# Statistics of the first mamba block's layer norm, pinned behind the projection of the second block

## The chip, the cores and the metric

The kernel runs on one core of a Trainium2 chip. The metric is the time on the device in microseconds (us) of one launch; runs are given with their median. A core has five engines with queues of their own, each of which executes in order: TensorE (PE in the profile, its weight loads PEld), VectorE (DVE), ScalarE (ACT), GpSimd (POOL) and SyncE (SP), which here mostly issues DMA transfers. Engines wait for each other by semaphores. Matmuls write into PSUM, of which the kernel uses eight banks of 128 x 512 float32 in turn.

## The reference

Two sequences of 1024 tokens with 512 features pass four layers. After each, the input is added and the row normalised. The first layer is a Mamba-2 mixer; only it and its layer norm matter here:

```python
def _layernorm(x, axis=-1, eps=1e-05):
    m = jnp.mean(x, axis=axis, keepdims=True)
    v = jnp.var(x, axis=axis, keepdims=True)
    return (x - m) / jnp.sqrt(v + eps)
...
zxbcdt = jnp.einsum('bld,di->bli', hidden_states, W_in)     # gate, xBC, dt
xBC = jax.nn.silu(conv)                                     # causal, 4 taps
h = h * dA_t[:, :, None, None] + (dt_t[:, :, None] * x_t)[..., None] * B_t[:, None, None, :]
y = jnp.einsum('bhpn,bn->bhp', h, C_t)                      # one scan step
y = y * jax.nn.silu(gate)
y = y * jax.lax.rsqrt(var + EPS) * norm_w
return jnp.einsum('bld,do->blo', y, W_out)
...
x = _layernorm(x + _L0_attn_ref(x, ...), axis=-1)
x = _layernorm(x + _L0_ffn_ref(x, ...), axis=-1)
x = _layernorm(x + _L1_attn_ref(x, ...), axis=-1)           # gated linear recurrence
x = _layernorm(x + _L1_ffn_ref(x, ...), axis=-1)            # SwiGLU
```

## The kernel before

The 2048 tokens are worked on in four blocks of 512 (`TB`). A block's rows `X[b]` lie as four tiles of 128 tokens by 512 features (`NJ` = 4). The mamba layer of a block has these stages, each a Python generator whose steps are woven together:

- `head(b)` makes `xT`, the block with features on partitions. For blocks 2 and 3 a DMA brings blocks of 32 x 32 and VectorE turns them (`turn_blocks`, L270, four instructions). Then `pbc` (L387) projects to B, C and dt, ScalarE copies the result, VectorE convolves it, and a DMA lays dt out by rows (`turn`, L404) for the softplus chain.
- `project(b)` makes the inner channels `px` (L366), convolves them on VectorE (L292, three taps each), and makes the decay matrices `L`: ScalarE copies a row-broadcast decay into a PSUM bank `pl` (L566), and VectorE scans it (L572). GpSimd multiplies by the Gram matrix (L587).
- `recur(b)` goes over four chunks of 128 tokens: transposes `pxt` (L668), their product with dt `dtx` (L670), the outputs `py` (L691 from the state, L699 from inside the chunk), the new state `pst` and `H` (L709, L716, L723), and the sum into `xc` (L730).
- `gates(b)` makes the eight gate projections `pg`; `gate(b)` applies them.
- `conclude(b)` projects to the output (`po`, L764, one group of 16 TensorE instructions for each 128 tokens), adds the residual (L779), and at its end normalises the block (`layernorm`) and stores it (`store_rows`).

`layernorm` issues for each of four tiles a statistics instruction on VectorE (L279, `bn_stats`) and one that turns it into mean and variance (L280, `bn_aggr`); then a square root on ScalarE (L282), a reciprocal (L283) and four instructions (x - mean) * rs on VectorE (L285).

The blocks overlap: `conclude(0)` is the filling between the steps of `project(1)`, and what is left of it is woven into `recur(1)`, together with the gates of block 1 and the head of block 2:

```python
fill, plan = conclude(b - 1, before), (0, 0, 2, 0, 2, 0, 2, 2)
...
weave(project(b, st), fill, plan, rest=False)
weave(recur(b, H, st), alternate(itertools.chain(fill, g), ahead), (3,) * NJ)
```

The order on each engine is not the order of these calls. Only the very first part is in the written order (`manual_schedule`); otherwise a scheduler places instructions by its own costs, and may bring one forward as soon as its inputs are there. An instruction given to `tc.keep_in_program_order` stays behind what was issued before it on its engine and is not brought forward. The four transposes of `xT` in `head` are such instructions (`pinned=True`).

Of the kernel before, what the change touches and what calls it, by code (L numbers as in the profile page):

```python
# [18 lines left out]
NJ = TB // P  # L19
# [18 lines left out]
def model_kernel(ctx: ExitStack, tc: tile.TileContext, t: dict, out: bass.AP):  # L38
    nc = tc.nc
# [20 lines left out]
    def bank(name):  # L60
        return ps.tile([P, 512], F32, tag="mm", name=name)
# [17 lines left out]
    def tokens():  # L79
        return op.tile([P, NJ, D], F32, tag="x", name="x", bufs=3)  # L80

    X = [tokens() for _ in range(3)]
# [170 lines left out]
    def store_rows(rows, x):  # L253
        nc.sync.dma_start(rows.rearrange("(j p) d -> p j d", p=P), x)
# [16 lines left out]
            if pinned:  # L271
                tc.keep_in_program_order(turned)

    def layernorm(x, n=NJ, engine=nc.vector):

        mv = sp.tile([P, NJ, 2], F32, tag="mv", name="mv")
        for j in range(n):
            st = sp.tile([P, 6], F32, tag="st", name="st", bufs=4)
            nc.vector.bn_stats(st, x[:, j, :])  # L279
            nc.vector.bn_aggr(mv[:, j, :], st)  # L280
        rs = sp.tile([P, NJ, 1], F32, tag="rs", name="rs")
        nc.scalar.activation(rs[:, :n], mv[:, :n, 1:2], AF.Sqrt, bias=eps)  # L282
        nc.vector.reciprocal(rs[:, :n], rs[:, :n])  # L283
        for j in range(n):
            engine.tensor_scalar(  # L285
                x[:, j, :], x[:, j, :], mv[:, j, 0:1], rs[:, j, :], ALU.subtract, ALU.mult
            )

# [467 lines left out]
    def conclude(b, st):  # L756


        xc, sums = st["xc"], st["sums"]
        rms = sp.tile([P, NJ], F32, tag="rms", name="rms")  # L760
        for j in range(NJ):
            po = bank("po")
            for m in range(NX):
                nc.tensor.matmul(  # L764
                    po, xc[:, m, j * P : (j + 1) * P], w_out[:, m, :],
                    start=(m == 0), stop=(m == NX - 1),
                )
                if m == NX // 2 - 1:
                    yield
            if j == 0:  # L770
                pss = bank("pss")
                for i in range(NJ):
                    nc.tensor.matmul(
                        pss[:, i : i + 1], sums[:, i * P : (i + 1) * P], ones,
                        start=True, stop=True,
                    )
                nc.scalar.activation(rms, pss[:, :NJ], AF.Sqrt, bias=eps, scale=1.0 / DI)
                nc.vector.reciprocal(rms, rms)
            nc.vector.scalar_tensor_tensor(  # L779
                X[b][:, j, :], po, rms[:, j : j + 1], X[b][:, j, :], ALU.mult, ALU.add  # L780
            )
            yield
        layernorm(X[b])
        store_rows(x_mid[b], X[b])

    def by_blocks(b, st):
# [4 lines left out]
    H, before, st = None, None, {}  # L791
# [10 lines left out]
    for b in range(NBLK):  # L802
        if b:
            g, coming = gates(b, st), {}
            fill, plan = conclude(b - 1, before), (0, 0, 2, 0, 2, 0, 2, 2)
            ahead = iter(())
            if b + 1 < NBLK:
                by_blocks(b + 1, coming)
                ahead = head(b + 1, coming)
            weave(project(b, st), fill, plan, rest=False)  # L810

            weave(recur(b, H, st), alternate(itertools.chain(fill, g), ahead), (3,) * NJ)
        else:
            turns = (ahead, g, ahead, g, g, g, ahead)
            weave(recur(b, H, st), (next(steps, None) for steps in turns), (2, 2, 1, 2))
            for m in range(NX):
                tc.keep_in_program_order(nc.gpsimd.tensor_scalar(
                    w_out[:, m, :], w_out[:, m, :], normw[:, m : m + 1], 1.0, ALU.mult, ALU.mult
                ))
        H = st["H"]  # L820
        gate(b, st)
        before, st = st, coming
    before_last.close()
    last = (conclude(NBLK - 1, before), first_layer.close)


# [39 lines left out]
    def later_layers(exact, last=None):  # L866
# [82 lines left out]
        def linear(b):  # L949
# [41 lines left out]
            for j in range(NJ):  # L991
                nc.vector.scalar_tensor_tensor(
                    X[b][:, j, :], o[:, j, :], f[:, j : j + 1], X[b][:, j, :],
                    ALU.mult, ALU.add,
                )
            layernorm(X[b], engine=nc.gpsimd)
            if b:
                store_rows(x_lin[b], X[b])
# [44 lines left out]
        with tc.tile_pool(name="rec" + suffix, bufs=1, side="right", reuse_waits="tile") as rp:  # L1043
# [91 lines left out]
            def project_back(b, y):  # L1135
                for j in range(NJ):
                    po = bank("po")
                    for k in range(NK):
                        nc.tensor.matmul(  # L1139
                            po, y[:, k, j * P : (j + 1) * P], w1[4][:, k, :],  # L1140
                            start=(k == 0), stop=(k == NK - 1),
                        )
                    r = rp.tile([P, D], F32, tag="t2", name="r1", bufs=4)
                    nc.vector.tensor_tensor(r, po, bout, ALU.add)
                    nc.gpsimd.tensor_tensor(X[b][:, j, :], X[b][:, j, :], r, ALU.add)  # L1145

                if b + 1 < NBLK:
                    layernorm(X[b])
                    store_rows(x_rec[b], X[b])
# [277 lines left out]
```

## Time and profile before

| | |
|---|---|
| median of 3 runs | 1121.71 us (1121.63 to 1123.01) |
| the profiled execution | 1122.32 us, its span 1120.5 us |
| PE busy | 1102.6 us, 98% of the span |
| DVE busy | 704.6 us, 63% |
| ACT, POOL busy | 453.6 us and 366.5 us |
| mean granted TensorE clock | 0.997 |

Times in the profile are microseconds from the start of the span, which is from the first to the last instruction. A row of the timeline gives start, duration, engine, line and operation, then the tiles written and read, the shapes and how many instructions are merged into it; in brackets, how long the engine stood idle before it and whose work ended that. `conclude(0)` ends within 111 and 171 us: the statistics of this layer norm stand at 136.5, 138.1, 154.5 and 163.4, and its last normalising instruction just before 170.7.

### The profile page before, as it was taken

The page shows a single profiled execution, that of the slowest core. Times are in us where ns is not written, and L with a number is a line of the kernel's source. Part 1 is how long each engine was busy: PE and PEld are TensorE (multiplying, and loading weights), DVE is VectorE, ACT ScalarE, POOL GpSimd, SP SyncE. Part 2 cuts the span into 40 slices and gives each one's busy share as a digit, 9 for nine tenths or more (in the row PEclk, how much of TensorE's full clock was granted, in tenths as well). Part 3 has the DMA queues.
Part 4 walks back from the last instruction along what each step waited for, and adds up shares of the span by engine and source line. Part 5 has one row for each costly group of instructions (what it writes and reads, how often), then busy time and mean ns, then how long its engine had stood idle before and what let it go on. Part 6 is the DMA issues. An engine that isn't in the chain of part 4 may idle for free.

```text
span 1120.5 us, 12075 instructions
## 1 busy us (share of the span) xinstructions
PE 1102.6 (98%) x4450; PEld 664.5 (59%) x4450; DVE 704.6 (63%) x1266; ACT 453.6 (40%) x692; POOL 366.5 (33%) x347
## 2 busy tenths in 40 slices
PE   9999999999999999999999999999999999999996
PEld 5455445445544555645444444447888888888885
DVE  5989897697869676874646438184238865325224
ACT  3334633463454233556644372553223224224223
POOL 1547471465248340453433231236411001001000
PEclk9999999999999999999999999999999999999999
DMA  9005302801220138246540001304654002100001
GB/s 325 19 11 119 95 1 92 206 1 38 82 105 0 39 125 224 57 103 151 112 76 8 30 1 38 38 0 130 193 100 75 1 1 59 17 1 29 9 1 41
DMA packets 122059, 77.04 MB, mean 69 GB/s; under 512 B 94512, under 2 KB 95312, under 8 KB 120456
## 3 DMA queue, kind: packets, MB, share of 16 engines
q1 hardware_dynamic: 120792, 75.77, 25.9%
q8 instruction: 37, 0.61, 0.2%
q10 hardware_dynamic: 976, 0.39, 0.1%
q14 instruction: 30, 0.25, 0.1%
q0 software_dynamic: 224, 0.02, 0.0%
HBM read 59.95 MB, written 16.02 MB: 68 GB/s over the span
## 4 chain that ended last, share of the span: by engine, by line
PE 82%; DVE 10%; ACT 4%; issue 1%; POOL 1%; DMA 1%; SPq 0%; DVEq 0%; ACTq 0%; POOLq 0%
PE pgu L1024 20%; PE p L1050 19%; PE po L1250 10%; PE pg L366 9%; PE px L366 7%; PE po L764 6%; PE po L1139 2%; PE py L699 2%; PE po L968 2%; DVE L L572 2%; DVE acc L292 2%; PE pxt L668 1%; POOL x L1145 1%; DVE st L279 1%; PE pbc L387 1%
## 5 line engine op out<-in xcount | busy, mean ns | idle before, releaser
L1035 DVE SCALAR_TENSOR_TENSOR h<-pgu,L_ffn_up_scale,sg 128x512 f32<-128x512 f32 x63 | 47.1, 748 | 126.5 <-PE pgu L1024 122.7
L764 PE MATMUL po<-w_out,xc 128*128 128x512 f32 x256 | 114.2, 600 | 2.2 <-DVE L L572 2.2
L366 PE MATMUL px<-xT,w_in 128*128 128x512 f32 x256 | 114.6, 597 | 0.0
L587 POOL TENSOR_TENSOR L<-L,gm 128x512 f32<-128x512 f32 x64 | 93.0, 1483 | 64.8 <-DVE bdec L582 38.3
L366 PE MATMUL pg<-xT,w_in 128*128 128x512 f32 x256 | 113.5, 594 | 0.0
L1050 PE MATMUL p<-xT,w 128*128 128x512 f32 x256 | 111.1, 592 | 1.0 <-ACT xT L248 1.0
L1050 PE MATMUL p<-cv,w 128*128 128x512 f32 x256 | 110.8, 592 | 0.0
L1024 PE MATMUL pgu<-wF__4239,wg 128*128 128x512 f32 x256 | 101.7, 397 | 0.0
L1024 PE MATMUL pgu<-lo__4240,wg 128*128 128x512 f32 x256 | 100.8, 394 | 0.0
L1024 PE MATMUL pgu<-lo__4240,wu 128*128 128x512 f32 x256 | 100.7, 393 | 0.0
L1024 PE MATMUL pgu<-wF__4239,wu 128*128 128x512 f32 x256 | 100.7, 393 | 0.0
L1250 PE MATMUL po<-wd,hh 128*128 128x512 f32 x252 | 98.3, 396 | 0.3 <-POOL wg L911 0.3
L1250 PE MATMUL po<-wd,hl 128*128 128x512 f32 x252 | 98.2, 396 | 0.2 <-DVE hl L1039 0.2
L1034 ACT ACTIVATE sg<-pgu,L_ffn_gate_scale 128x512 f32<-128x512 f32 x63 | 43.4, 689 | 125.6 <-PE pgu L1024 125.5
L764 PEld LDWEIGHTS po<-w_out,xc 128*128 128x128 f32 x256 | 49.0, 192 | 64.3 <-issue 57.1
L1038 ACT CAST hh<-h 128x512 fp32r<-128x512 f32 x63 | 39.1, 621 | 114.6 <-DVE h L1035 114.4
L1050 PEld LDWEIGHTS p<-xT,w 128*128 128x128 f32 x256 | 48.5, 190 | 60.8 <-issue 57.6
L1050 PEld LDWEIGHTS p<-cv,w 128*128 128x128 f32 x256 | 48.6, 190 | 60.4 <-issue 59.1
L366 PEld LDWEIGHTS px<-xT,w_in 128*128 128x128 f32 x256 | 47.5, 190 | 57.5 <-issue 56.2
L366 PEld LDWEIGHTS pg<-xT,w_in 128*128 128x128 f32 x256 | 47.3, 190 | 54.2 <-issue 53.3
L292 DVE SCALAR_TENSOR_TENSOR acc<-xpad,cols,acc 128x512 f32<-128x512 f32 x72 | 67.2, 935 | 18.9 <-ACT acc L336 14.1
L1368 POOL TENSOR_TENSOR x<-x,r 128x512 f32<-128x512 f32 x12 | 15.2, 1300 | 194.2 <-DVE r L1367 194.2
(291 smaller groups left out, 1929.2 us busy)
## 6 DMA issues: line engine op xcount, KB each, us to landing
L<-decays SPq DMA_DIRECT2D x12, 1024.0 KB, 7.1
x_mid<-x SPq DMA_DIRECT2D x4, 1024.0 KB, 4.3
x<-x_mid SPq DMA_DIRECT2D x4, 1024.0 KB, 8.1
st<-in_L_ffn_gate_w_dram SPq DMA_DIRECT2D x8, 512.0 KB
st<-in_L_ffn_up_w_dram SPq DMA_DIRECT2D x8, 512.0 KB, 3.9
st<-in_L_ffn_down_w_dram SPq DMA_DIRECT2D x8, 512.0 KB, 4.1
x_rec<-x SPq DMA_DIRECT2D x4, 1024.0 KB, 4.7
x<-_attn_hidden_states_dram SPq DMA_DIRECT2D x3, 1024.0 KB
```

What stands on the lines that cost most here:

```text
L292: tap = nc.vector.scalar_tensor_tensor(acc, xpad[:, k : k + TB], w[:, k : k + 1], acc, ALU.mult, ALU.add)
L366: nc.tensor.matmul(pm[:n, :], w_in[:, k, lo : lo + n], xT[:, k, :], start=(k == 0), stop=(k == NK - 1),)
L572: nc.vector.tensor_tensor_scan(L[:, h, :], pl, id4.rearrange("p j t -> p (j t)"), 0.0, ALU.mult, ALU.add)
L587: nc.gpsimd.tensor_tensor(L[:, h, :], L[:, h, :], st["gm"], ALU.mult)
L699: nc.tensor.matmul(pys[i][hh * HD : (hh + 1) * HD, q, :], dtx[q][:, 2 * i + hh, :], L[:, h, s], start=(first and q == 0), stop=(q == 1), s ...
L764: nc.tensor.matmul(po, xc[:, m, j * P : (j + 1) * P], w_out[:, m, :], start=(m == 0), stop=(m == NX - 1),)
L1024: nc.tensor.matmul(pm, w[g][:, k, cols], x[:, k, :], start=(k == 0 and x is pieces[0]), stop=(k == NK - 1 and x is pieces[-1]),)
L1034: nc.scalar.activation(sg, pgu[0], AF.Silu, scale=gs[:, m : m + 1])
L1035: nc.vector.scalar_tensor_tensor(h, pgu[1], us[:, m : m + 1], sg, ALU.mult, ALU.mult)
L1038: nc.scalar.copy(halves[0], h)
L1050: nc.tensor.matmul(pm, w1[i][:, k, m * P : (m + 1) * P], rhs[:, k, :], start=(k == 0), stop=(k == NK - 1),)
L1250: nc.tensor.matmul(po[j], x[:, j * P : (j + 1) * P], wd[m // GK][:, m % GK, :], start=(m == 0 and x is h[0]), stop=(m == NF - 1 and x is h ...
```

## The change

`layernorm` gets a parameter `pinned`. With it, each `bn_stats` is kept in program order. `conclude` sets it for block 0 alone. A second new parameter, `last`, is never given and changes nothing.

```diff
-    def layernorm(x, n=NJ, engine=nc.vector):
+    def layernorm(x, n=NJ, engine=nc.vector, last=None, pinned=False):
...
         for j in range(n):
             st = sp.tile([P, 6], F32, tag="st", name="st", bufs=4)
-            nc.vector.bn_stats(st, x[:, j, :])
+            stats = nc.vector.bn_stats(st, x[:, j, :])
+            if pinned:
+                tc.keep_in_program_order(stats)
             nc.vector.bn_aggr(mv[:, j, :], st)
...
         for j in range(n):
-            engine.tensor_scalar(
+            (last if last and j == n - 1 else engine).tensor_scalar(
                 x[:, j, :], x[:, j, :], mv[:, j, 0:1], rs[:, j, :], ALU.subtract, ALU.mult
             )
...
-        layernorm(X[b])
+        layernorm(X[b], pinned=b == 0)
         store_rows(x_mid[b], X[b])
```

In program order these statistics come after the whole projection of block 1 and the first steps of its recurrence. On VectorE the changed program has, after the scans and convolutions of `project(1)`: the residual of the last 128 tokens, `dtx` of chunk 0, the sums into `xc`, `H`, `dtx` of chunk 1, then four times `bn_stats` and `bn_aggr`, the reciprocal, the four normalising instructions, and then the four transposes of `xT`. Before, the first two pairs stood between the scans of `project(1)`, the third ahead of its last convolution, and the fourth after `dtx` of chunk 0. On ScalarE the square root moves from ahead of the first SiLU of the gates `pg` to between the first and the second. On TensorE, two of the `py` matmuls of chunk 1 now stand between the four parts of `pbc`. On SP, `turn` of block 2 now stands ahead of the load of the fourth block's `x` (L376). Lines below `layernorm` are three higher in the changed file.

## The prediction

> **What bounds the kernel now.** I read the page first, then the waits of TensorE, the timelines of TensorE and VectorE around the first layer norm, and last the granted clock in short windows. The page:
>
> ```profile
> span 1120.5 us, 12075 instructions
> PE 1102.6 (98%) x4450; PEld 664.5 (59%) x4450; DVE 704.6 (63%) x1266; ACT 453.6 (40%) x692; POOL 366.5 (33%) x347
> PEclk9999999999999999999999999999999999999999
> ```
>
> TensorE is busy for 98% of the span, so time moves only where TensorE stands still or runs slower. Moving VectorE work around is worth something only where TensorE waits for VectorE. The waits of TensorE (line, releaser, total, times, longest) hold one such place that matters:
>
> ```profile
> PE po L764 <- DVE L L572: 2.2, 2, 1.9
> ```
>
> The timelines show it: TensorE first, then VectorE, then one ScalarE row (start, duration, what; idle before in brackets).
>
> ```profile
> 142.37 8.83 PE L764 MATMUL po<-w_out,xc 128*128 128x512 f32 x16 [1.95 <-DVE L L572]
> ...
> 166.72 7.03 PE L366 MATMUL pg<-xT,w_in 128*128 128x512 f32 x16
> 173.69 1.93 PE L387 MATMUL pbc<-xT,w_bc 128*48 128x256 f32 x16
> ```
> ```profile
> 136.47 0.70 DVE L279 BATCH_NORM_STATS2 st<-x 128x6 f32<-128x512 f32 x1
> 137.21 0.18 DVE L280 BATCH_NORM_AGGREGATE mv<-st 128x2 f32<-128x6 f32 x1
> 137.31 0.72 DVE L779 SCALAR_TENSOR_TENSOR x<-po,rms,x 128x512 f32<-128x512 f32 x1
> 138.06 0.69 DVE L279 BATCH_NORM_STATS2 st<-x 128x6 f32<-128x512 f32 x1
> ...
> 138.88 4.55 DVE L572 TENSOR_TENSOR_SCAN L<-pl,id 128x512 f32<-128x512 f32 x4
> ...
> 168.69 0.68 DVE L670 TENSOR_TENSOR dtx<-pxt,tk 128x512 f32<-128x512 f32 x1
> 169.29 1.45 DVE L285 TENSOR_SCALAR x<-x,mv,rs 128x512 f32<-128x512 f32 x3
> 170.65 2.48 DVE L270 STREAM_TRANSPOSE xT<-xT 128x512 f32<-128x512 f32 x4
> ...
> 271.07 0.18 DVE L283 RECIPROCAL rs<-rs 128x4 f32<-128x4 f32 x1 [0.36 <-ACT rs L282]
> 271.28 1.92 DVE L285 TENSOR_SCALAR x<-x,mv,rs 128x512 f32<-128x512 f32 x4
> 273.11 2.48 DVE L270 STREAM_TRANSPOSE xT<-xT 128x512 f32<-128x512 f32 x4
> ```
> ```profile
> 136.80 2.13 ACT L566 COPY pl<-L 128x512 f32<-128x512 f32 x4
> ```
>
> What to see: two statistics pairs (L279, L280) stand on VectorE just ahead of four scans (L572). The third scan ends at 142.32 and frees the PSUM bank that the output projection `po` wants; TensorE, idle since 140.42, starts at 142.37. And that group of 16 matmuls takes 8.83 us where the same group takes about 6.87 elsewhere in the chain of waits. The windows say why (stretch, length, PE busy, PEld, DVE, ACT, POOL, then the granted clock):
>
> ```profile
> 140.09:143.50 3.41, 1.46 (x4) 0.65 (x4) 3.38 (x4) 3.27 (x7) 1.71 (x3) 1.00 0.00 0
> 143.50:146.92 3.42, 3.42 (x5) 1.38 (x5) 3.42 (x5) 0.00 (x0) 2.95 (x3) 0.50 0.00 0
> 1109.47:1112.88 3.41, 2.08 (x9) 1.33 (x8) 3.23 (x9) 2.96 (x10) 1.55 (x2) 1.00 0.20 75
> ```
>
> A stretch with PE busy for 1.46 of 3.41 us was followed by one at half clock. The third row, busy for 2.08, was followed by full clock. The PEclk row of the page is too coarse to show this.
>
> **The change part by part.**
>
> *Taken away from the projection.* Four pairs leave their places. A pair takes 0.84 us of VectorE (136.47 to the next instruction's start at 137.31). Only the first two stand ahead of the wait. Without them the scans could start 2 x 0.84 = 1.68 earlier, but the first scan needs ScalarE's first copy into `pl`: four copies start at 136.80, each 0.58 long, so the first is there at 137.38 and the scan starts at 137.41, not 138.88. VectorE gains 1.47, the third scan ends at 140.85, and the hold of TensorE shrinks from 1.95 to about 0.48. Gain 1.47. VectorE stays busy from here to 153, so what follows on it moves as a block. The third pair (154.49) stands ahead of the last convolution; I give its removal 0.2. Together 1.6 to 1.7.
>
> *The clock.* A hold of 0.48 leaves that window busy for about 2.9 of 3.41 us, above the 2.08 that kept full clock. So the half-clock stretch goes: 8.83 - 6.87 = 1.96, of which about 0.2 would be lost again waiting for the last convolution; I take 1.8. It counts only in executions that had it.
>
> *Put back later.* All four pairs, the reciprocal and the four normalising instructions (L285) now stand on VectorE behind the operands of the second chunk (`dtx`, L670) and ahead of the four block transposes (L270) that make the third block's `xT`. TensorE needs these for `pbc` (L387) and executes in order. In times of the profile before: `dtx` ends at 169.37 and may gain 0.15 (it is tied to TensorE's `pxt` and to GpSimd), so 169.2. Four pairs: 4 x 0.84 = 3.36, to 172.6. Square root on ScalarE and reciprocal, by the row at 271.07 (idle 0.36, then 0.21 to the next start): normalising starts at 173.15. Four of them take 1.83 (271.28 to 273.11): transposes start at 174.98. The first takes 0.70, the next follow every 0.6: 175.68, 176.28, 176.88, 177.47. TensorE is through with the gate matmuls `pg` at 173.69, so it stands for 2.0 us, then runs a quarter of `pbc` (0.43) for each transpose. The last quarter starts at 177.50 instead of 174.98: 2.52 late. In the order of the changed program two of the eight state products (`py`, L691) now lie between the quarters, which gives back 0.16. Loss 2.35. Before, the first transpose ended at 171.35 and the gate matmuls covered 2.34 us more; now it ends 4.33 later, so that cover is gone and 2.0 sticks out. Bounds: 1.1 if all that VectorE is spared ahead of `dtx` (a pair, the reciprocal, one normalising step: 0.84 + 0.1 + 0.46 = 1.4 instead of 0.15) reached the transposes; 2.9 if GpSimd's multiplications slow a few of the moved instructions (L723 took 1.12 beside them, 0.62 without).
>
> *What else moves.* ScalarE's square root goes between the two SiLUs of `pg`, with its two table loads of 1.28 us as before; the first load runs while VectorE still makes statistics, and the second SiLU comes at about 174.2 instead of 173.79. The bank it empties is wanted some 5 us later. On SP, the store of the normalised block is issued some 4 us later; the load of the fourth block into `x` (L376), which waits for that store, now stands behind `turn<-rpad` (L404), which no longer waits in the queue behind that load. Readers of the stored block come at 456 us. The chain behind `pbc` (ScalarE copy, convolution, `turn`) moves with `pbc`; the next `dtx` on VectorE ends at 183.39 for a use at 187.23, so its reordering by up to 0.4 us is hidden by `pg`. All cost nothing while those 3.8 us last.
>
> *Sum.* In executions that pay for the clock equally before and after: -1.6 + 2.35 = +0.75. Against the profiled execution, which had the half-clock stretch: 1122.32 (span 1120.5, 1.8 around it) - 1.6 - 1.8 + 2.35 = 1121.3, or 1123.0 if the new hold is answered by half clock too. The profiled execution lies 0.6 above the median 1121.71, and the runs spread over 1.4 us, which is about one half-clock stretch.
>
> **A rule against the row.** The row first: 1.46 busy of 3.41, then clock 0.50. The Trainium skill, "TensorE: Matmul & The Clock Gate", section "What's actually happening", has the clock halved after at least one idle window of about 3.4 us, and calls the window free-running, not reset by the kernel. By its idle window, neither the hold of 1.95 nor the new one of 2.0 would be answered: the sum would be +0.75 in every execution. By the row both can be; the row decides that. What the page adds and one trace can't show is the free phase: whether a hold of 2 us falls into one window is then chance. With a deciding point half way (1.7 idle), a hold of 1.95 is caught in (3.41 + 1.95 - 2 x 1.7) / 3.41 = 57% of phases, by my estimate from these rows. The new hold, with the small gaps between the quarters, is caught about as often. That speaks against this change: it swaps one hold for another of the same length, instead of removing it.
>
> **The rivals.**
> 1. *Both executions in one clock state: +0.75*, 1122.5. For: the two holds are alike (1.95 and 2.0). Against: phases may differ. Chance 0.54; this is my forecast.
> 2. *The old half-clock stretch goes and no new one comes*: the hold at `pbc` is cut by quarters of `pbc` and may fall across two windows. -1.6 - 1.8 + 2.35 = -1.05, 1120.7. Chance 0.2. Even so it stays within 0.2%; only if VectorE reaches the transposes as early as the lower bound of the loss does it come to -2.3 (chance 0.1 for faster).
> 3. *The clock gate at `pbc`, slower*: the median run before had no half-clock stretch and the new one has. Place: the window holding the 2.0 us before `pbc`; price 1.8; it decides where that window's busy time falls below something between 2.08 and 1.46 us. +0.75 + 1.8 = +2.55, 1124.3. Against: the trace of before has one. Chance 0.2.
> 4. *The statistics are hidden in both places*: 0, 1121.7, if the `pbc` hold were covered as the old one would be. The row of `pg` ending at 173.69 speaks against. Chance 0.06.
>
> **How the numbers follow.** 0.2% of this time is 2.2 us, about what a measurement of this kernel can tell from no change. Predicted 1122.5. The range takes in the case at 1120.7 with its bounds down to 1120.2, and rival 3 up to 1124.6. Slower by over 0.2%: rival 3 (0.2) and the upper bound of the loss in case 1 with some clock cost (0.1): 0.3. Faster: 0.1. Within: 0.6.
>
> **What would show it.** Right: VectorE's scans at 137.4 directly behind L779; TensorE's wait for L572 down to about 0.5 us; `po` at 6.9 us; then a new wait of TensorE's `pbc` (L390 in the changed file) for the transposes (L270) of about 2 us, and `pbc` drawn out from 1.9 to some 2.3 us. Wrong: the wait at `pbc` under 1 us, or the scans not earlier by over a microsecond, or a TensorE wait after `pbc` that is not there now.

## The result

The changed kernel takes 1125.55 us in the median of 10 executions (1123.25 to 1126.96), the kernel before 1122.28 (1121.09 to 1123.49, 10): ratio 1.0027, 95% interval [1.0019, 1.0035]. It is 3.3 us slower, where 0.75 was forecast, and lies above the range. The profiled execution is one of the quickest of the changed kernel, 1123.25 us. That is already part of the answer: its executions spread over 3.7 us.

The page of the changed kernel and the top of its TensorE waits (line, releaser, total, times, longest):

```profile
span 1121.4 us, 12076 instructions
PE 1101.5 (98%) x4450; PEld 663.9 (59%) x4450; DVE 705.3 (63%) x1266; ACT 453.2 (40%) x692; POOL 365.7 (33%) x347
```
```profile
PE pbc L390 <- issue: 2.0, 1, 2.0
...
PE po L767 <- DVE L L575: 1.3, 2, 0.8
```

The old hold ahead of `po` is down: of the 1.3 us in its row, 0.50 lie at the scans, and 0.82 at 127 us, ahead of anything that the change touches. A new hold of 2.0 us stands ahead of `pbc`. The waits view puts it down to "issue", since TensorE's queue stands there in a semaphore instruction of its own; the timelines show for what. TensorE of the changed kernel (start, duration, what; idle before in brackets):

```profile
141.58 7.13 PE L767 MATMUL po<-w_out,xc 128*128 128x512 f32 x16 [0.50 <-DVE L L575]
...
164.35 7.03 PE L369 MATMUL pg<-xT,w_in 128*128 128x512 f32 x16
173.41 0.64 PE L390 MATMUL pbc<-xT,w_bc 128*48 128x256 f32 x4 [2.02 <-issue]
173.97 0.48 PE L694 MATMUL py<-cdec,H 32*128 32x128 f32 x2
174.39 0.64 PE L390 MATMUL pbc<-xT,w_bc 128*48 128x256 f32 x4
174.96 0.48 PE L694 MATMUL py<-cdec,H 32*128 32x128 f32 x2
175.37 1.07 PE L390 MATMUL pbc<-xT,w_bc 128*48 128x256 f32 x8
176.37 0.71 PE L694 MATMUL py<-cdec,H 32*128 32x128 f32 x12
177.01 1.97 PE L702 MATMUL py<-L,dtx 128*64 128x128 f32 x32
```

VectorE of the same execution:

```profile
138.07 4.57 DVE L575 TENSOR_TENSOR_SCAN L<-pl,id 128x512 f32<-128x512 f32 x4 [0.18 <-ACT pl L569]
...
166.31 0.68 DVE L673 TENSOR_TENSOR dtx<-pxt,tk 128x512 f32<-128x512 f32 x1
166.92 0.68 DVE L280 BATCH_NORM_STATS2 st<-x 128x6 f32<-128x512 f32 x1
...
170.56 0.18 DVE L286 RECIPROCAL rs<-rs 128x4 f32<-128x4 f32 x1 [0.36 <-ACT rs L285]
170.77 1.91 DVE L288 TENSOR_SCALAR x<-x,mv,rs 128x512 f32<-128x512 f32 x4
172.60 2.48 DVE L270 STREAM_TRANSPOSE xT<-xT 128x512 f32<-128x512 f32 x4
```

The scans now wait for ScalarE's copy, not for statistics. `po` starts after 0.50 us and takes 7.13 instead of 8.83. Then statistics, reciprocal and normalising stand between `dtx` and the transposes; the first transpose ends at 173.30, and `pbc` starts at 173.41. In this execution the clock was full from here to the end of the matmuls. From the first quarter of `pbc` to the inner products (`py`, L702) 3.60 us pass; before it was 2.52 (173.69 to 176.21):

```profile
173.69 1.93 PE L387 MATMUL pbc<-xT,w_bc 128*48 128x256 f32 x16
175.55 0.73 PE L691 MATMUL py<-cdec,H 32*128 32x128 f32 x16
176.21 1.97 PE L699 MATMUL py<-L,dtx 128*64 128x128 f32 x32
```

This execution lies 0.66 later than that of before, ahead of anything that the change touches: VectorE from 95 us on (the last section tells what is known of it), TensorE from 127 us on, where it waits for a scan for 0.82 instead of 0.23. The 0.66 is taken off in comparisons with the trace of before.

### The profile page after: what moved, and what is told of

It reads as the page before. It is cut to its first block, busy times and chain, and to the rows that moved or that the text cites. A ratio compares the mean times of both kernels' runs of the same rounds, so it can differ in the third digit from the quotient of the medians.

```text
span 1121.4 us, 12076 instructions
## 1 busy us (share of the span) xinstructions
PE 1101.5 (98%) x4450; PEld 663.9 (59%) x4450; DVE 705.3 (63%) x1266; ACT 453.2 (40%) x692; POOL 365.7 (33%) x347
## 4 chain that ended last, share of the span: by engine, by line
PE 81%; DVE 11%; ACT 4%; issue 2%; POOL 1%; DMA 1%; SPq 0%; DVEq 0%; ACTq 0%; POOLq 0%
PE pgu L1027 20%; PE p L1053 19%; PE po L1253 10%; PE pg L369 9%; PE px L369 7%; PE po L767 4%; DVE acc L295 3%; PE po L1142 2%; PE py L702 2%; DVE L L575 2%; PE po L971 2%; PE pxt L671 1%; POOL x L1148 1%; PE py L694 1%; PE pbc L390 1%
```

## The experiments

**again: the changed kernel once more.**

> The changed kernel once more, for a second profile and the spread of its runs. Theory A (the clock gate answers the new hold ahead of pbc): runs fall into groups, a quiet one about 2 us above the quiet runs of before (about 1123.3) with one hold of 2 us and full clock, and one some 3 us higher (about 1126.5) whose profile shows half clock within 7 us after the hold at pbc. Theory B (a plain longer wait, no clock): the runs spread evenly and a profile of a slow run shows full clock from 120 to 200 us but a hold at pbc of 4 us and more.

Measured: median 1125.13 of 6 (1123.26 to 1126.49), ratio 1.0029 [1.0017, 1.0041]; before had a median of 1122.19 over 49 executions (1120.79 to 1123.57). The profiled one, 1123.26, again shows the hold of 2.0 and full clock. With the executions of the first measurement, those at 1123.3 have a mean granted clock of 0.997 and those above 1124.1 one of 0.994 to 0.996. So the spread goes with the clock; where the clock was low these numbers don't say.

**look1, look2, look3: more profiles of the same program.** No edit.

> The changed kernel for one more profile, to see an execution in which the clock gate answers. The runs so far lie between 1123.3 and 1127.0 with a granted clock of 0.997 down to 0.994. Theory A1: an execution above 1125 shows two stretches of 3.41 us at half clock in a row behind the hold at pbc, since the short pbc and py matmuls leave the first of them little busier; cost about 3.2. Theory A2: one such stretch (1.7) and a second one elsewhere. If it is a quiet one (1123.3): full clock throughout, as in the profile already seen.

> As look1: one more profile of the changed kernel; half clock twice in a row behind pbc (A1), or once there and once elsewhere (A2), or none if the time is about 1123.3.

> As look1: one more profile of the changed kernel; half clock twice in a row behind pbc (A1), or once there and once elsewhere (A2), or none if the time is about 1123.3.

Measured: 1123.31, 1125.13 and 1126.14 us. The three stand for three cases, to be read in windows set on the clock's own steps (stretch, length, PE, PEld, DVE, ACT, POOL busy, granted clock, DMA). The steps within a trace lie a whole number of 3.413 us apart, so they can be laid through the hold also where the clock does not change. look2:

```profile
171.04:174.45 3.41, 1.39 (x9) 0.55 (x10) 3.41 (x8) 1.39 (x2) 0.00 (x0) 1.00 0.24 91
174.45:177.86 3.41, 3.41 (x15) 1.34 (x14) 0.65 (x2) 0.00 (x0) 0.00 (x0) 0.50 0.58 216
177.86:181.28 3.42, 3.42 (x64) 2.82 (x63) 1.49 (x3) 1.55 (x3) 0.18 (x1) 1.00 0.28 27
```

look3:

```profile
171.22:174.63 3.41, 1.78 (x12) 0.89 (x12) 3.31 (x7) 0.65 (x2) 0.00 (x0) 1.00 0.47 176
174.63:178.04 3.41, 3.41 (x24) 1.75 (x24) 0.00 (x0) 0.98 (x3) 0.18 (x1) 0.50 0.36 132
178.04:181.45 3.41, 3.41 (x33) 3.21 (x32) 2.73 (x5) 0.62 (x2) 0.00 (x0) 0.50 0.41 104
```

and, from the profile of the result, where the hold lasts from 171.39 to 173.41 and a step of the clock falls just ahead of its end:

```profile
169.84:173.25 3.41, 1.54 (x4) 0.38 (x2) 2.97 (x9) 2.22 (x4) 0.00 (x0) 1.00 0.00 0
```

look1 has full clock and 1123.31. In look2 the window that holds the whole hold is followed by one half-clock stretch, and the time is 1.8 higher. In look3 two stretches follow each other, and the time is 2.8 higher, although the 0.66 of the early part is absent from it; with that, 3.5. Both had the clock full elsewhere, so A2 is out, and A1 is seen in look3 but not in look2: the new hold is answered by half clock, in one stretch or in two. Of the 19 executions of the changed program in all, five lie at 1123.3 and fourteen above 1124.1, seven of these above 1126; that these seven had two stretches is read from their times and from look3 alone.

**unsplit: the parts of `pbc` kept together.**

```diff
-                        nc.tensor.matmul(
+                        read = nc.tensor.matmul(
                             pys[i][:, q, :], H[w, q, :], cdec[w, q, s], start=(q == 0), stop=False,
                             skip_group_check=True,
                         )
+                        if b == 1 and c == 1:
+                            tc.keep_in_program_order(read)
```

> The changed kernel with the eight state products of chunk 1 of block 1 kept behind pbc, so that the four parts of pbc follow each other as in the kernel before. The transposes come as late as in the changed kernel. Theory C (mixing pbc with the state products costs TensorE): pbc to the start of the inner products of chunk 1 shrinks from 3.6 to about 2.9 us, and the quiet runs fall by 0.7. If the mixing costs nothing: no difference. Theory A: the hold of 2 us stays, so the slow runs stay too, median about 1125.

Measured: median 1122.85 of 13 (1121.74 to 1124.43), ratio 1.0007 [0.9998, 1.0015]. TensorE of its profile, and the weight loads of the last three quarters of `pbc`:

```profile
173.57 2.37 PE L390 MATMUL pbc<-xT,w_bc 128*48 128x256 f32 x16 [2.02 <-issue]
175.88 0.73 PE L694 MATMUL py<-cdec,H 32*128 32x128 f32 x16
176.53 1.97 PE L704 MATMUL py<-L,dtx 128*64 128x128 f32 x32
```
```profile
174.12 0.17 PEld L390 LDWEIGHTS pbc<-xT,w_bc 128*48 128x48 f32 x4 [0.37 <-DVE xT L270]
174.71 0.17 PEld L390 LDWEIGHTS pbc<-xT,w_bc 128*48 128x48 f32 x4 [0.42 <-DVE xT L270]
175.30 0.17 PEld L390 LDWEIGHTS pbc<-xT,w_bc 128*48 128x48 f32 x4 [0.42 <-DVE xT L270]
```

The hold is the same 2.02, and from `pbc` to the inner products it is 2.96 instead of 3.60: mixing two state products between the quarters costs 0.64 us. The transposes pace `pbc` here, 0.59 us apart; in the changed kernel the quarters follow 0.98 apart, later than the transposes would let them. The median fell by more, 2.3, where theory A expected it to stay at about 1125: the slow executions are still there (five from 1123.5 to 1124.4) but fewer and less slow, and none reaches 1126.

**look_unsplit.** One more profile of unsplit.

> The kernel unsplit for one more profile. Its runs lie between 1121.7 and 1124.4, the slower ones only 1.3 us above the others. If its time is above 1123.4: one stretch of half clock behind pbc, not two. If below: none.

Measured: 1124.02, and one half-clock stretch; the next has full clock.

```profile
173.78:177.20 3.42, 3.42 (x24) 1.56 (x24) 1.33 (x3) 0.29 (x1) 0.00 (x0) 0.50 0.79 293
```

It costs 1.2 us here (1124.02 against the 1122.84 of the profile with full clock), as the quarters of `pbc` have to wait for the transposes in any case. No second one has been seen without the mixing, and no execution of unsplit lies more than 1.6 above its median. How a second stretch is brought about is told below as open.

**filler: TensorE kept at work in the hold.**

```diff
+        if b == 2:
+            for _ in range(4):
+                tc.keep_in_program_order(
+                    nc.tensor.matmul(pm, ident, w_in[:, 0, :TB], start=True, stop=True)
+                )
```

> The changed kernel with four float32 matmuls of 128x512 on constants in the place where TensorE stands still ahead of pbc (1.7 us at full clock, into the bank that pbc then overwrites). It also keeps the parts of pbc together. Theory A (clock gate): the hold stays under 0.5 us of idle time, no half clock follows, and the spread upwards goes: all runs within 1.5 us of the quiet ones, median about 1122.5, 3 us below the changed kernel. Theory B (plain longer wait): the extra matmuls fill the wait but transposes are as late as before, so nothing is gained: median as the changed kernel, 1125.5. Theory C (the parts of pbc cost the time): gains 0.7 as unsplit does, no more, 1124.8.

Measured: median 1123.46 of 21 (1122.70 to 1124.15), ratio 1.0012 [1.0006, 1.0019]. The four matmuls took 3.60 us, not 1.7, as each float32 matmul is two instructions of 0.43: they outlast the hold by some 1.3 us, and the parts of `pbc` follow unbroken. Still it is 1.7 to 2.1 below the changed kernel, and none of 21 executions lies above 1124.2. TensorE does useless work for longer than it waited, and the median falls. That speaks for the clock and against a plain wait (B); but two things were changed.

**filler2: two such matmuls, on top of unsplit.** The diff against unsplit is that of filler with `range(2)`.

> The kernel unsplit with two float32 matmuls of 128x512 on constants ahead of pbc, which is all that differs: 4 instructions of 0.43 us, 1.7 us, inside the hold of 2.0. Theory A (clock gate): the quiet runs are those of unsplit (about 1122.7 less or more by its early 0.6), idle time ahead of pbc about 0.3 us, and the group about 1124 goes; no half clock. Theory B (the hold itself is all): the same times as unsplit, 1121.7 to 1124.4, slow group included.

Measured: median 1122.69 of 13 (1121.71 to 1123.03), ratio 1.0003 [0.9994, 1.0011]. TensorE:

```profile
171.38 1.88 PE L391 MATMUL pbc<-w_in,ident 128*128 128x512 f32 x4
173.53 2.42 PE L395 MATMUL pbc<-xT,w_bc 128*48 128x256 f32 x16 [0.26 <-DVE xT L270]
```

Here the idle time has its releaser named: it ended with the transposes (L270). `pbc` starts as late as in unsplit, so nothing useful is done earlier; the group of unsplit from 1123.5 to 1124.4 (five of 13) is gone, the highest being 1123.03; none of these 13 shows a mean granted clock under 0.997, where six of unsplit show 0.996. Both theories gave the same quickest times; only the clock theory gave the end of that group.

**late: the statistics one step further back, behind the transposes.**

```diff
             turn_blocks(xT, pinned=True)
+            if b == 2:
+                layernorm(X[0], pinned=True)
+                store_rows(x_mid[0], X[0])
...
-        layernorm(X[b], pinned=b == 0)
-        store_rows(x_mid[b], X[b])
+        if b:
+            layernorm(X[b])
+            store_rows(x_mid[b], X[b])
```

> The statistics of the first layer norm pinned one step further back, behind the four transposes of the third block instead of ahead of them; the rest as in the changed kernel. If the order against the transposes is the whole loss (theory A with its hold, or B): no hold at pbc, the scans keep their gain of 1.45 us, no half clock in either place, median about 1120, 2 us below before. If the late statistics cost elsewhere (convolution of pbc, dtx of chunk 2): median at or above 1122.3.

Measured: median 1119.95 of 20 (1119.27 to 1120.53), ratio 0.9980 [0.9973, 0.9987]: faster than both. TensorE, then VectorE:

```profile
141.80 7.13 PE L770 MATMUL po<-w_out,xc 128*128 128x512 f32 x16 [0.49 <-DVE L L578]
...
171.55 1.93 PE L393 MATMUL pbc<-xT,w_bc 128*48 128x256 f32 x16
```
```profile
167.16 2.47 DVE L270 STREAM_TRANSPOSE xT<-xT 128x512 f32<-128x512 f32 x4
169.56 0.64 DVE L280 BATCH_NORM_STATS2 st<-x 128x6 f32<-128x512 f32 x1
```

The gain at the scans is as in the changed kernel, and `pbc` starts without a hold, its quarters together. The statistics fill time in which VectorE stood still before, waiting for ScalarE's part of the convolution of `pbc` (4.24 us before, 0.60 here). No execution of 20 shows a clock under 0.997.

**late_both: the same for the second layer norm.** In `conclude` the condition is `b > 1`, and in `head` the condition on `b` goes: `layernorm(X[b - 2], pinned=True)`.

> The kernel late with the same move for the second layer norm as well (its statistics behind the transposes of the fourth block). In block 2 the trace of before has no hold of TensorE in the projection, so if a hold is what makes the move pay: no difference from late, 1119.95 within 0.5. If freeing VectorE of statistics among the scans pays by itself: lower by about 1.5, 1118.5. If the moved statistics delay something there: higher.

Measured: median 1120.14 of 13 (1119.22 to 1120.61), ratio 0.9978 [0.9969, 0.9986], as late. In block 2 TensorE had no hold to lose; in the kernel before its rows at these scans follow each other without idle time:

```profile
240.30 7.03 PE L366 MATMUL px<-xT,w_in 128*128 128x512 f32 x16
247.17 7.03 PE L764 MATMUL po<-w_out,xc 128*128 128x512 f32 x16
```

So fewer VectorE instructions among the scans do not pay by themselves; where there was a hold, the move paid.

## Why the prediction was wrong

*The gain at the scans: right in mechanism, 0.4 too large.* The scans stand behind ScalarE's copies, the hold is 0.50 (forecast 0.48), and `po` runs at full clock. Up to the start of the gate matmuls the changed kernel gained 166.72 - (164.35 - 0.66) = 3.03 on the profile of before, against 1.6 + 1.8 = 3.4. The hold gave 1.45 and the clock 8.83 - 7.13 = 1.70 (the prediction's 8.83 - 6.87 = 1.96 took a row's duration against a distance between starts). The 0.2 for the third pair did not come: from `pxt` to the gate matmuls it now takes 5.50 instead of 5.38, with a wait of 0.20 for ScalarE.

*The hold at `pbc`: right in place and length.* 2.02 against 2.0. The way to it held as well: four pairs in 3.3 us, 0.36 to the reciprocal, transposes 0.6 apart. The shift of `dtx` by 0.15 did not come, and the pairs were as much shorter (0.80 for 0.84): two small errors that cancel.

*The mixing of `pbc` and `py`: wrong in sign.* The step took the two state products between the quarters of `pbc` for a credit of 0.16. They cost 0.64, by unsplit, and `pbc` is drawn out to 2.96 (173.41 to 176.37) where 2.3 was said. The loss was therefore 2.02 + (3.60 - 2.52) = 3.10, not 2.35, and beyond the upper bound of 2.9. Executions with full clock before and after are then apart by about 3.10 - 1.45 + 0.12 = 1.8, where the sum said 0.75.

*The clock: right in kind, wrong in price, and this weighed most.* The prediction gave the new hold the chances and the price of the old one: answered in 57% of phases, 1.8 each, so that the two cancel and rival 3 had a chance of 0.2. For the kernel before that is borne out: of its 49 executions 24 lie between 1122.4 and 1123.6, the others between 1120.8 and 1122.2, and none is high enough for two stretches. After, 14 of 19 pay, too few to tell from 57%, but seven of these pay for two stretches, some 3.4. The term that failed is the price of 1.8: the answer to the new hold can last 6.83 us instead of 3.41.

*The sum.* About 1.8 from hold and mixing, and some 1.1 to 1.5 more from the clock, as the difference to 2.9 (again) and 3.3 (the result). The part of the clock is a remainder; that there is one is shown by filler2, look2 and look3, its mean size is not measured apart.

*When a hold is answered.* The prediction put the deciding point between 1.46 and 2.08 us of busy time in a window. Read in windows on the clock's steps, busy time alone does not decide: in look3 a window busy for 1.78 was answered, and in the profile of the result one busy for 1.54 was not. Two readings fit. One is that short matmuls count for less: the first window holds `pbc` and `py` matmuls, the second only full gate matmuls. The other is that the stretch that counts ends a little before the clock steps. Windows laid 0.3 us earlier, look3 first, then the result:

```profile
170.92:174.33 3.41, 1.48 (x10) 0.66 (x10) 3.41 (x7) 0.95 (x2) 0.00 (x0) 1.00 0.38 142
169.54:172.95 3.41, 1.84 (x5) 0.53 (x3) 2.97 (x8) 2.52 (x4) 0.00 (x0) 1.00 0.00 0
```

| window at the hold | PE busy, on the steps | PE busy, 0.3 us earlier | next stretch |
|---|---|---|---|
| look_unsplit | 1.38 | 1.38 | half clock |
| look2 | 1.39 | 1.39 | half clock |
| before | 1.46 | 1.46 | half clock |
| look3 | 1.78 | 1.48 | half clock |
| the result | 1.54 | 1.84 | full clock |
| look1 | 1.61 | 1.91 | full clock |
| unsplit | 2.15 | 1.84 | full clock |

In the right-hand column one deciding point, between 1.48 and 1.84, sorts all of them, and it lies inside the prediction's range. A shift of 0.2 to 0.4 does so for every window at full clock in the twelve traces; 0.1 and 0.5 do not. The shift was chosen after the rows were seen and no run tests it, so neither reading is shown.

*The rule weighed.* The prediction set a rule of the Trainium skill ("TensorE: Matmul & The Clock Gate", "What's actually happening") against the row: that the clock is halved after an idle window of about 3.4 us. As a condition it is too strict here: the longest of these holds was 2.04 us (look1), and holds of 2.02 and 2.03 were answered by half clock in look2, look3 and look_unsplit. The free phase is borne out: the same program had none, one and two stretches.

*What else was said to cost nothing* (ScalarE's square root, the store and the load on SP, the chain behind `pbc`) shows no wait of TensorE in the profile after. The first reader of the stored block comes at 411.9 us in the trace of before, not at 456; that is as harmless.

Open: what makes the second stretch. In look2, look3 and look_unsplit TensorE is busy in the whole of the first half-clock stretch by its records; in look3 alone another follows. That stretch holds 8 instructions of `pbc` and 16 of `py`, in look2 it is 12 and 3, in look_unsplit 16 and 8. That the 32-row matmuls of `py` count for less would fit; no run here sets the size of matmuls and the phase of the clock apart.

## What to carry to other kernels

Work moved off one wait lands somewhere in the same queue: before pinning an instruction late, look at what stands next behind it on its engine and who waits for that; here the place behind the four transposes, not ahead of them, made a loss of 3 us a gain of 2. A hold of TensorE of 2 us costs its length and, by chance of phase, half clock on what follows, so judge it with the matmuls around it and in several executions, not in one profile. Where a hold can't be taken away, matmuls on constants inside it may keep the clock up; here two did so at no cost (filler2).

## What the runs showed of the hardware

The half-clock stretches among the matmuls lasted 3.41 us (before, look2, look_unsplit) or 6.83 (look3), at a phase that differs from execution to execution. They followed windows with TensorE busy for 1.38 to 1.78 of 3.41 us by the clock's steps, while windows busy for 1.54 and 1.61 were followed by full clock.

Going from matmuls that use 128 rows by 48 columns (`pbc`) to one of 32 by 128 (`py`, state) and back cost 0.54 us each time: two such products lengthen the way from `pbc` to the inner products by 3.60 - 2.52 = 1.08. Unsplit saved only 0.64 of it, as the transposes then hold the quarters apart. How much of the 0.54 is the change of shape and how much the product itself was not measured.

The kernels, before included, have a second, smaller spread of 0.6 us that has nothing to do with the change. One small VectorE instruction takes 0.81 or 0.33 us, in the result's profile and in look3:

```profile
93.85 0.81 DVE L483 TENSOR_SCALAR work<-work,by_hj 64x128 f32<-64x128 f32 x1
```
```profile
93.87 0.33 DVE L483 TENSOR_SCALAR work<-work,by_hj 64x128 f32<-64x128 f32 x1
```

GpSimd scales `w_out` at the same time (L817 of the kernel before). Every trace here has one value or the other, nothing between (0.33 in before, look3 and filler, 0.81 or 0.82 in the other nine), and what follows on VectorE starts up to 0.66 later. That the two engines get in each other's way there is a guess: GpSimd's work is there in the quick traces too, and no run took it away.
